# Attention scores of two query tiles as seven partial products, with another order of values and outputs

## The chip, the cores and the metric

The kernel runs on one core of one Trainium2 chip. It is a block of four layers (a gated linear attention, a feed-forward layer with 8-bit weights, a softmax attention, the same feed-forward layer again) on an input of 2 x 1024 tokens with 512 features, in float32. The metric is the device time of one execution in microseconds (us); lower is better. Three runs of the kernel before took 958.06, 958.42 and 961.21 us.

The core has a matrix engine (TensorE, PE in the profile; PEld is its weight load), a vector engine (VectorE, DVE), a scalar engine (ScalarE, ACT), GpSimd (POOL) and SyncE (SP), which issues most DMAs. Each works through its own instructions in order; semaphores make one wait for another. PSUM, the memory that TensorE writes, has eight banks of 128 x 512 float32.

## The reference

Only the third layer, the softmax attention, is touched. With `x` the normalised tokens:

```python
def _L0_attn_b_ref(x, W_q, W_k, W_v, W_o):
    scale = 1.0 / jnp.sqrt(jnp.asarray(x.shape[-1], x.dtype))
    Q = jnp.einsum('bsd,de->bse', x, W_q)
    K = jnp.einsum('bsd,de->bse', x, W_k)
    V = jnp.einsum('bsd,de->bse', x, W_v)
    scores = jnp.einsum('bqe,bke->bqk', Q, K) * scale
    attn = jax.nn.softmax(scores, axis=-1)
    out = jnp.einsum('bqk,bke->bqe', attn, V)
    return jnp.einsum('bse,ed->bsd', out, W_o)
```

Each of the two batches has 1024 tokens that attend to all 1024 tokens of their batch. The kernel folds the weights: with M = W_q W_k^T the scores are (x M) x^T, and with W_v W_o the last two products become one. So there are four products per batch: queries x M, scores, values x W_v W_o, outputs.

## The kernel before

Numbers are kept in two parts: a high part that TensorE's fast float32 format holds exactly, and a low part with the rest. `split` (L83) makes them: ScalarE casts the high part (L85), VectorE subtracts it for the low part (L86). A product of two such operands takes three matmuls, high x high, high x low, low x high (`mm3`, L95 to L98).

A batch has eight query tiles of 128 tokens and eight key tiles. `xTs[b, s]` holds half s of a batch's tokens transposed, 512 features as four blocks k of 128 partitions by 512 tokens, high and low part in one slot each. "Slots" are twelve buffers of 128 x 2048 (L39) shared by all stages. `wm` and `wvo` (L847 to L853) hold M and W_v W_o, loaded once from DRAM at the start of the stage.

- `q_proj` (L855) makes 512 queries: for each of four feature blocks 4 x 3 matmuls, split into `qh`, `ql`.
- `scores_b` (L874) makes the scores of one query tile: for each half of the keys 4 x 3 matmuls into one PSUM bank, the maximum of each half (L885), the negated scaled maximum `nm`, exponentials `pe` with their sums, the reciprocal `ri`.
- `probs_T` (L908) transposes the probabilities: VectorE transposes 32 x 32 blocks (L927), and a store to DRAM (`p_d`, L929) and four loads (L937) move the blocks to their places; then they are split into `pth` and `ptl`. The last tile of all is transposed on TensorE instead (L913 to L925).
- `out_b` (L946) makes the outputs of one tile, 8 x 3 matmuls, scales them by `ri`, adds the residual that it loads, and stores `x3`.
- `v_tile` (L958) makes 128 rows of values.

The order is written out in the loops at L986 to L1013: queries of the first half, four value tiles, scores of tile 0, four more value tiles, and then for each tile i the scores of i + 1, the probabilities of i and the outputs of i - 1. Other work is hung between: layer norms of the next tokens (`ln_steps`, which normalise, transpose in 32 x 32 blocks and move the blocks by DMA, L185 to L208), and the splits of the next tokens (`ln_split`, L210). `behind(last)` asks the scheduler to place such work after the last exponentials. The framework's scheduler then fixes each engine's order at build time.

The feed-forward layers already work by seven products. `combine` (L238) takes four quarters of the tokens of a pair of groups (B11, B12, B21, B22: two groups of 512 tokens by two halves of the features), forms the sums T1 to T4, and splits them; `products` (L304) multiplies them with prepared weights; in `ffn`, X, Y, Z and V are four PSUM banks that are added to each other on VectorE (L772 to L778) between the first four products and the last three. `ffn`'s second pass over layer "f" also carries the first norms and splits of the attention's tokens, given as its last argument (L838).

In the tail of each pass, `ffn` makes the outputs of eight token tiles: 22 matmuls each (L816, L817), a scaling and an addition on VectorE (L818, L819), a residual load before (L809) and a store after (L823). `xr` has two buffers.

## Time and profile before

| | |
|---|---|
| median of three runs | 958.42 us (958.06 to 961.21) |
| the profiled execution: its run, its span | 960.34 us, 958.5 us |
| TensorE busy (matmuls; weight loads) | 944.9 us (99%); 782.4 us (82%) |
| VectorE busy | 669.1 us (70%) |
| ScalarE busy | 372.6 us (39%) |
| GpSimd busy | 211.3 us (22%) |
| score matmuls `psc` | 384, 489.4 to 717 us |
| output matmuls `pob` | 384, 517.1 to 734.8 us |
| query and value matmuls `pqb`, `pvb` | 192 each |

The attention stage runs from about 463 to 735 us. The profile is one execution, taken by the hardware. In its rows the first number is the start or the sum of the busy time; matmul durations are from start to modelled end, and successive matmuls overlap. In a window's answer each engine has a pair: busy time and number of instructions, in the order PE, PEld, DVE, ACT, POOL, followed by the granted clock of TensorE, the share of the DMA engines and GB/s. A list of waits gives who waited on which line for whom, then the sum in us, how often, and the longest. The DMA share of the stage's window is 0.55.

### The profile page before, as it was taken

To read this page: it belongs to the slowest core of one execution; us is meant where nothing else is said; L and a number is where in the kernel's file an instruction comes from. 1 tells how busy PE (TensorE), PEld (TensorE's weight loads), DVE (VectorE), ACT (ScalarE), POOL (GpSimd) and SP (SyncE) were. 2 spreads that over 40 slices of the span, in tenths; PEclk is the share of its full clock that TensorE was granted. 3 is DMA by queue.
4 is the path that set the end of the run, shared out by engine and by line. 5 is a ranking of instruction groups with operands and counts; after the bars stand their busy time and mean duration, and the time that the engine had idled before them with its cause. 6 is when DMAs were issued, how large, how long until landed. Compare 5 with 4: busy or idle time off the path is not lost.

```text
span 958.5 us, 13125 instructions
## 1 busy us (share of the span) xinstructions
PE 944.9 (99%) x4450; PEld 782.4 (82%) x4450; DVE 669.1 (70%) x1361; ACT 372.6 (39%) x719; POOL 211.3 (22%) x310
## 2 busy tenths in 40 slices
PE   8999999999999999999999999999999999999998
PEld 7788788888888878888888877888888888888887
DVE  7766767768999699786437458246565986976655
ACT  4643424345565344454122224113233444434421
POOL 5432323333455011110001443104000121001100
PEclk9999999999999999999999999999999999999999
DMA  9536456574988457635505778427567762563112
GB/s 315 170 101 149 149 128 189 170 196 144 336 331 265 124 188 274 182 79 182 192 22 134 159 169 200 107 66 161 127 141 262 268 201 45 186 234 140 39 58 96
DMA packets 219250, 160.06 MB, mean 167 GB/s; under 512 B 154992, under 2 KB 170672, under 8 KB 219184
## 3 DMA queue, kind: packets, MB, share of 16 engines
q1 hardware_dynamic: 217136, 155.03, 54.1%
q0 software_dynamic: 2048, 4.20, 1.9%
q8 instruction: 35, 0.57, 0.2%
q14 instruction: 31, 0.25, 0.1%
HBM read 102.66 MB, written 41.84 MB: 151 GB/s over the span
## 4 chain that ended last, share of the span: by engine, by line
PE 65%; DMA 5%; DVE 5%; SPq 1%; POOL 1%; issue 0%; ACT 0%; DVEq 0%; ACTq 0%; POOLq 0%
PE pog L817 4%; PE pog L816 4%; PE pVg L312 4%; PE pZg L312 4%; PE pXg L312 4%; PE pVf L312 3%; PE pZf L312 3%; PE pXf L312 3%; PE pof L816 3%; PE pof L817 3%; PE pob L98 3%; PE pob L97 2%; PE pob L96 2%; PE psc L96 2%; PE psc L98 2%; PE psc L97 2%
## 5 line engine op out<-in xcount | busy, mean ns | idle before, releaser
L816 PE MATMUL pog<-wdg,hsg 128*128 128x512 f32 (+1 forms) x165 | 60.3, 375 | 0.0
L817 PE MATMUL pog<-wdg,hsg 128*128 128x512 f32 (+1 forms) x165 | 60.3, 376 | 0.0
L817 PE MATMUL pof<-wdf,hsf 128*128 128x512 f32 x154 | 59.4, 391 | 0.8 <-DVE hsf L86 0.8
L894 ACT ACTIVATE pe<-psc,nm 128x512 f32<-128x512 f32 x32 | 21.7, 684 | 98.1 <-DVE nm L889 98.1
L816 PE MATMUL pof<-wdf,hsf 128*128 128x512 f32 x154 | 59.2, 390 | 0.0
L98 PE MATMUL pob<-vh,ptl 128*128 128x512 f32 x128 | 50.3, 393 | 0.7 <-DVE ptl L86 0.7
L98 PE MATMUL psc<-xh_b,ql 128*128 128x512 f32 x128 | 50.6, 395 | 0.0
L96 PE MATMUL psc<-xh_b,qh 128*128 128x512 f32 x128 | 50.6, 395 | 0.0
L97 PE MATMUL psc<-xT_b,qh 128*128 128x512 f32 x128 | 50.5, 395 | 0.0
L96 PE MATMUL pob<-vh,pth 128*128 128x512 f32 x128 | 50.1, 392 | 0.2 <-ACT pth L85 0.2
L97 PE MATMUL pob<-vl,pth 128*128 128x512 f32 x128 | 49.9, 390 | 0.0
L86 POOL TENSOR_TENSOR hsg<-sgg,hsg 128x128 fp32r<-128x128 f32 x40 | 17.6, 462 | 146.0 <-ACT hsg L85 146.0
L117 POOL TENSOR_TENSOR rs_b<-ve_b,mhalf 128x1 f32<-128x1 f32 x16 | 10.9, 685 | 167.3 <-DVE ve_b L115 150.8
L312 PE MATMUL pVg<-T_g,wcg 128*128 128x512 f32 x176 | 46.9, 390 | 0.0
L312 PE MATMUL pVf<-T_f,wcf 128*128 128x512 f32 x176 | 46.6, 390 | 0.0
L312 PE MATMUL pXg<-B_g,wcg 128*128 128x512 f32 x176 | 46.6, 390 | 0.0
L312 PE MATMUL pXf<-B_f,wcf 128*128 128x512 f32 x176 | 46.0, 391 | 0.4 <-DMA wcf<-wc 0.4
L885 DVE TENSOR_REDUCE mx<-psc 128x1 f32<-128x512 f32 x32 | 21.9, 687 | 30.0 <-PE psc L98 29.8
L117 POOL TENSOR_TENSOR rs_g<-ve_g,mhalf 128x1 f32<-128x1 f32 x16 | 9.0, 573 | 144.7 <-DVE ve_g L115 128.2
L312 PEld LDWEIGHTS pXf<-B_f,wcf 128*128 128x128 f32 x176 | 32.9, 188 | 7.5 <-DMA wcf<-wc 0.8
L312 PEld LDWEIGHTS pVf<-T_f,wcf 128*128 128x128 f32 x176 | 33.1, 188 | 6.9
L312 PEld LDWEIGHTS pVg<-T_g,wcg 128*128 128x128 f32 x176 | 33.1, 188 | 6.9
(298 smaller groups left out, 2658.9 us busy)
## 6 DMA issues: line engine op xcount, KB each, us to landing
wcg<-wc SPq DMA_DIRECT2D x22, 896.0 KB, 5.4
wc<-wcf SPq DMA_DIRECT2D x11, 896.0 KB, 5.4
wcf<-wc SPq DMA_DIRECT2D x11, 896.0 KB, 6.1
p<-py SPq DMA_DIRECT2D x15, 512.0 KB, 3.4
ptl<-p SPq DMA_DIRECT2D x60, 128.0 KB, 3.1
xin_a<-in_x SPq DMA_DIRECT2D x16, 256.0 KB, 4.2
xra<-in_x SPq DMA_DIRECT2D x16, 256.0 KB, 3.5
row<-cl SPq DMA_DIRECT2D x16, 256.0 KB, 3.9
```

Of the source, the lines that this page charges most:

```text
L86: return c.ins, (eng or nc.vector).tensor_tensor(lo, src, hi.bitcast(F32), ALU.subtract).ins
L96: nc.tensor.matmul(ps, lhs_hi, rhs_hi, start=first, stop=False)
L97: nc.tensor.matmul(ps, lhs_hi, rhs_lo, start=False, stop=False)
L98: return nc.tensor.matmul(ps, lhs_lo, rhs_hi, start=False, stop=last).ins
L117: rsqrt[:] = [nc.gpsimd.tensor_tensor(rs, ve, mhalf, ALU.pow).ins]
L312: nc.tensor.matmul(ps, w[:, m, k * P : (k + 1) * P], o[:, s, k, :], start=first and k == 0 and s == 0, stop=k == 1 and s == 1, skip_group_ ...
L816: nc.tensor.matmul(ps, hs[i][0][:, j], wd[j][:, ds], start=j == 0, stop=False)
L817: nc.tensor.matmul(ps, hs[i][1][:, j], wd[j][:, ds], start=False, stop=j == KH - 1)
L885: nc.vector.tensor_reduce(mx[:, s : s + 1], ps, AX.X, ALU.max)
L894: nc.scalar.activation(pe[:, s * 512 : (s + 1) * 512], pS[s], AF.Exp, bias=nm, scale=SC, accum_out=rs[:, s : s + 1],).ins
```

## The change

A pair of query tiles (256 queries) is treated as a 2 x 2 block matrix: A11, A12 are the first tile's two halves of the features, A21, A22 the second tile's. The keys of a batch are the four quarters B11, B12, B21, B22, which `combine` prepares as it does for the feed-forward layers, for which a list of steps of its own is added for nm == "b" (with B12 split too, since queries and values read all four quarters). The eight block products become seven, P1 to P7:

- `q_proj` no longer splits: ScalarE copies the queries to float32 in a slot.
- `q_operands` forms S1 to S4 from the float32 queries on VectorE and splits A11, S1, S2, S3 (early) and A12, A22, S4 (late) into high and low parts, each 128 x 256.
- `scores_head` makes P1, P6, P5, P7 into X, Y, Z, V, and ScalarE and VectorE add them; `scores_tail` adds P2, P3, P4, and then takes the softmax of both tiles. One of the four score halves (`up`) now lies in SBUF.
- `cycle` is one pair's head, work in between, and tail. The order is new: in batch 0 all eight value tiles first, then the queries; in batch 1 the first queries, the outputs 5 to 7 of batch 0, then the values. `wvo` is loaded once per batch, ahead of `wm` in batch 0. Outputs run behind the next pair's scores.
- The tile that TensorE transposes is now the last but one; the last goes through DRAM.

```diff
@@ combine
+        if nm == "b":
+
+            return [
+                lambda: (begin(), part("B11", "B11")),
+                lambda: part("B21", "B21"),
+                lambda: part("B12", "B12"),
+                lambda: part("B22", "B22"),
+                lambda: less("B11", "B12", "B11"),
+                lambda: part("T1", "B11"),
+                lambda: less("B12", "B22", "B12"),
+                lambda: part("T3", "B12"),
+                lambda: less("B22", "B22", "B11"),
+                lambda: part("T2", "B22"),
+                lambda: less("B21", "B21", "B22"),
+                lambda: part("T4", "B21"),
+            ]
@@ ffn(x1, x2, "f", ...)
-        (ln_steps(x2, "b", 0) + ln_steps(x2, "b", 1), ln_split("b", 0) + ln_split("b", 1)),
+        (ln_steps(x2, "b", 0) + ln_steps(x2, "b", 1), combine("b", 0)),
@@ attention stage
+        def q_proj(b, g, ms):
+            if ms[0] == 0:
+                qs[b, g] = slot(f"q{b}{g}", F32).rearrange("p (k c) -> p k c", k=KD)
+            for m in ms:
...
+                nc.scalar.copy(qs[b, g][:, m, :], ps)
+        def q_operands(b, n, late):
...
+            def part(nm, src):
+                o = b1.tile([P, 2, 2, P], F32R, tag=f"op{nm}", name=f"op{nm}_{b}{n}")
+                QA[b, n, nm] = o
+                split(o[:, 0], o[:, 1], src)
+
+            if late:
+                part("A12", A["A12"])
+                part("A22", A["A22"])
+                nc.vector.tensor_tensor(A["A12"], A["A12"], A["A11"], ALU.subtract)
+                part("S4", A["A12"])
+                return
+            s1 = b1.tile([P, 2, P], F32, tag="s1", name=f"s1_{b}{n}")
+            part("A11", A["A11"])
+            nc.vector.tensor_tensor(s1, A["A21"], A["A22"], ALU.add)
+            nc.vector.tensor_tensor(A["A21"], A["A11"], A["A21"], ALU.subtract)
+            nc.vector.tensor_tensor(A["A11"], s1, A["A11"], ALU.subtract)
+            part("S2", A["A11"])
+            part("S1", s1)
+            part("S3", A["A21"])
+
+        def score_product(ps, b, n, nm, first):
+            a_, x = {
+                "P1": ("A11", "B11"), "P2": ("A12", "B21"), "P3": ("S4", "B22"), "P4": ("A22", "T4"),
+                "P5": ("S1", "T1"), "P6": ("S2", "T2"), "P7": ("S3", "T3"),
+            }[nm]
+            o, w = QA[b, n, a_], XT["b", b, x]
+            for k in range(2):
+                for i, j in ((0, 0), (0, 1), (1, 0)):
+                    nc.tensor.matmul(
                         ps,
+                        o[:, i, k],
+                        w[:, j, k],
+                        start=first and k == 0 and i + j == 0,
+                        stop=k == 1 and i == 1,
+                        skip_group_check=nm != "P6",
                     )
...
+        def scores_head(b, n):
+            X, Y, Z, V = (psum(f"ps{x}{b}{n}") for x in "XYZV")
+            for ps, nm in ((X, "P1"), (Y, "P6"), (Z, "P5"), (V, "P7")):
+                score_product(ps, b, n, nm, True)
+            u2 = b1.tile([P, 512], F32, tag="u2", name=f"u2b{b}{n}")
+            nc.scalar.copy(u2, X)
+            nc.vector.tensor_tensor(u2, Y, u2, ALU.add)
+            up = bp.tile([P, 512], F32, tag="up", name=f"upb{b}{n}")
+            nc.scalar.copy(up, Z)
+            nc.vector.tensor_tensor(Z, Z, u2, ALU.add)
+            nc.vector.tensor_tensor(V, V, u2, ALU.add)
+            nc.vector.tensor_tensor(up, V, up, ALU.add)
+            heads[b, n] = X, Z, V, up
+
+        def scores_tail(b, n):
+            X, Z, V, up = heads.pop((b, n))
+            for ps, nm in ((X, "P2"), (Z, "P3"), (V, "P4")):
+                score_product(ps, b, n, nm, False)
+            last.clear()
+            softmax(b * NK + 2 * n, (X, Z))
+            softmax(b * NK + 2 * n + 1, (V, up))
@@ probs_T
-            if t == NT - 1:
+            if t == NT - 2:
@@ order of the stage
+        def cycle(b, n, between):
+            scores_head(b, n)
+            if n == 0:
+                q_operands(b, 0, True)
+            if n < 3 and n != 1:
+                q_operands(b, n + 1, False)
+            between()
+            if n == 1:
+                q_operands(b, 2, False)
+            scores_tail(b, n)
+            if n < 3:
+                q_operands(b, n + 1, True)
+
+        wvo = blocks(vo_d, "wvo0_")
+        wm = blocks(m_d, "wm")
         for b in range(NB):
+            nm, src, g = ("b", x2, 2) if b == 0 else ("g", x3, 0)
+            norm = ln_steps(src, nm, g) + ln_steps(src, nm, g + 1)
             if b == 0:
+                for kt in range(NK):
+                    v_tile(0, kt)
+                do(norm, 4)
+                q_proj(0, 0, range(KD))
+                q_operands(0, 0, False)
+                do(norm, 4)
+            else:
+                do(moving, 1)
+                out_b(0, 5)
+                q_proj(1, 0, range(KD))
+                q_operands(1, 0, False)
+                do(moving, 4)
+                out_b(0, 6)
+                do(norm, 2)
+                out_b(0, 7)
+                wvo = blocks(vo_d, "wvo1_")
+                for kt in (4, 5, 6, 7):
+                    v_tile(1, kt)
+                do(moving, 2)
+                for kt in range(4):
+                    v_tile(1, kt)
+                do(norm, 2)
+                do(moving, 4)
+                do(norm, 4)
+            cycle(b, 0, lambda: q_proj(b, 1, (0, 1)))
+            do(norm, 2)
+            for i in (0, 1):
+                probs_T(b, i)
+            do(norm, 2)
+            cycle(b, 1, lambda: q_proj(b, 1, (2, 3)))
+            do(norm, 4)
+            for i in (2, 3):
+                probs_T(b, i)
+            out_b(b, 0)
+            if b:
+                moving = combine("g", 0)
+                do(moving, 2)
+            cycle(b, 2, lambda: out_b(b, 1))
+            for i in (4, 5):
+                probs_T(b, i)
+            out_b(b, 2)
+            if b:
+                do(moving, 2)
+            else:
+                moving = combine("b", 1)
+                do(moving, 1)
+            cycle(b, 3, lambda: out_b(b, 3))
+            if b == 0:
+                for i in (6, 7):
+                    probs_T(b, i)
+                out_b(b, 4)
+        do(moving, 3)
+        out_b(1, 4)
+        for i in (6, 7):
+            probs_T(1, i)
+        do(moving, 3)
+        out_b(1, 5)
+        out_b(1, 6)
         wcs = [stationary(n, "g0") for n in range(2)]
-        ended = (out_b(NB - 1, NK - 1),)
+        ended = (out_b(1, 7),)
```

In the names below, X, Y, Z, V are the four banks of a pair, an output's number is its query tile, and "head" and "tail" are the two functions above. `do` takes the next steps of a list and places them behind the last exponentials.

More of the change, by code (lines that the diff above doesn't have):

```diff
@@ L846, in hybrid_block_kernel @@
         bp = bctx.enter_context(tc.tile_pool(name="attn_b", bufs=2))
-        wm, wvo = [], []
-        for dst, d, n in ((wm, m_d, "wm"), (wvo, vo_d, "wvo")):
-            two = [slot(f"{n}{m}") for m in range(2)]
-            for k in range(KD):
-                w = two[k // 2][:, k % 2 * 1024 : (k % 2 + 1) * 1024]
-                nc.sync.dma_start(out=w.bitcast(F32), in_=d[k])
-                dst.append(w)
-        def q_proj(xT, name):
-            xh, xl = xT
-            qh = b1.tile([P, KD, 512], F32R, tag="qh", name=f"qh{name}")
-            ql = b1.tile([P, KD, 512], F32R, tag="ql", name=f"ql{name}")
-            for m in range(KD):
-                ps = psum(f"pqb{name}_{m}")
-                for k in range(KD):
-                    mm3(
-                        ps,
-                        wm[k][:, m * P : (m + 1) * P],
-                        wm[k][:, 512 + m * P : 512 + (m + 1) * P],
-                        xh[:, k, :],
-                        xl[:, k, :],
-                        k == 0,
-                        k == KD - 1,
-                    )
-                split(qh[:, m, :], ql[:, m, :], ps)
-            return qh, ql
@@ L874, in scores_b, with blocks @@
-        def scores_b(b, i):
-            t = b * NK + i
-            qh, ql = qTs[b, i // ST]
-            cs = bass.ts(i % ST, P)
-            pS = []
-            mx = mp.tile([P, 2], F32, tag="mx", name=f"mx{t}")
-            for s in range(2):
-                xh, xl = xTs[b, s]
-                ps = psum(f"psc{t}_{s}")
-                for k in range(KD):
-                    mm3(ps, qh[:, k, cs], ql[:, k, cs], xh[:, k, :], xl[:, k, :], k == 0, k == KD - 1)
-                nc.vector.tensor_reduce(mx[:, s : s + 1], ps, AX.X, ALU.max)
-                pS.append(ps)
+        def blocks(d, name):
+            two = [slot(f"{name}{m}") for m in range(2)]
+            w = [two[k // 2][:, k % 2 * 1024 : (k % 2 + 1) * 1024] for k in range(KD)]
+            for x, src in zip(w, d):
+                nc.sync.dma_start(out=x.bitcast(F32), in_=src)
+            return w
@@ new lines, in tokens @@
+        def tokens(b, g, k):
+            o = XT["b", b, f"B{k // 2 + 1}{g + 1}"]
+            return o[:, 0, k % 2], o[:, 1, k % 2]
+        def q_proj(b, g, ms):
+            if ms[0] == 0:
+                qs[b, g] = slot(f"q{b}{g}", F32).rearrange("p (k c) -> p k c", k=KD)
+            for m in ms:
+                ps = psum(f"pqb{b}{g}_{m}")
+                ms_ = slice(m * P, (m + 1) * P), slice(512 + m * P, 512 + (m + 1) * P)
+                for k in range(KD):
+                    mm3(ps, wm[k][:, ms_[0]], wm[k][:, ms_[1]], *tokens(b, g, k), k == 0, k == KD - 1)
+                nc.scalar.copy(qs[b, g][:, m, :], ps)
@@ new lines, in q_operands @@
+        def q_operands(b, n, late):
+            A = {}
+            for i in range(2):
+                for j in range(2):
+                    c = (n % 2 * 2 + i) * P
+                    A[f"A{i + 1}{j + 1}"] = qs[b, n // 2][:, 2 * j : 2 * j + 2, c : c + P]
+            def part(nm, src):
[16 more added lines that the diff above has]
+            part("S3", A["A21"])
@@ new lines, in scores_tail, with softmax @@
+        def scores_tail(b, n):
[5 more added lines that the diff above has]
+            softmax(b * NK + 2 * n + 1, (V, up))
+        def softmax(t, halves):
+            mx = mp.tile([P, 2], F32, tag="mx", name=f"mx{t}")
+            for s, x in enumerate(halves):
+                nc.vector.tensor_reduce(mx[:, s : s + 1], x, AX.X, ALU.max)
@@ L891, in scores_b @@
             rs = mp.tile([P, 2], F32, tag="rsum", name=f"rsum{t}")
-            for s in range(2):
-                last[:] = [
-                    nc.scalar.activation(
-                        pe[:, s * 512 : (s + 1) * 512],
-                        pS[s],
-                        AF.Exp,
-                        bias=nm,
-                        scale=SC,
-                        accum_out=rs[:, s : s + 1],
-                    ).ins
-                ]
+            for s, x in enumerate(halves):
+                act = nc.scalar.activation(
+                    pe[:, s * 512 : (s + 1) * 512], x, AF.Exp, bias=nm, scale=SC, accum_out=rs[:, s : s + 1]
+                )
             ri = mp.tile([P, 1], F32, tag="ri", name=f"ri{t}")
             nc.vector.tensor_tensor(ri, rs[:, 0:1], rs[:, 1:2], ALU.add)
-            last.append(nc.vector.reciprocal(ri, ri).ins)
+            last[:] = act.ins, nc.vector.reciprocal(ri, ri).ins
             pes[t] = pe, ri
@@ L958, in v_tile @@
         def v_tile(b, kt):
-            xh, xl = xTs[b, kt // ST]
             cs = bass.ts(kt % ST, P)
@@ L962, in v_tile @@
             for k in range(KD):
+                xh, xl = tokens(b, kt // ST, k)
                 w = wvo[k]
-                mm3(ps, xh[:, k, cs], xl[:, k, cs], w[:, 0:512], w[:, 512:1024], k == 0, k == KD - 1)
+                mm3(ps, xh[:, cs], xl[:, cs], w[:, 0:512], w[:, 512:1024], k == 0, k == KD - 1)
             h_ = b1.tile([P, 512], F32R, tag=f"vh{kt}", name=f"vh{b}_{kt}")
@@ L968, in v_tile @@
             vs[b, kt] = h_, l_
-        xTs, qTs, pes, ptT, vs, last = {}, {}, {}, {}, {}, []
-        fill = [[[] for _ in range(NK)] for b in range(NB)]
-        for b, src, nm, g, its in (
-            (0, x2, "b", 2, (0, 0, 1, 1, 1, 1, 2, 2)),
-            (0, x2, "b", 3, (2, 2, 3, 3, 3, 3, 4, 4)),
-            (0, x3, "g", 0, (5, 5, 6, 6, 7, 7, 7, 7)),
-            (1, x3, "g", 1, (0, 0, 1, 1, 1, 1, 2, 2)),
-        ):
-            for t, step in zip(its, ln_steps(src, nm, g)):
-                fill[b][t].append(step)
@@ L981, in hybrid_block_kernel, with do @@
-        fill[0][6][:0] = ln_split("b", 2)
-        moving = combine("g", 0)
-        for n in range(10):
-            fill[1][(3, 3, 4, 4, 4, 5, 5, 5, 6, 6)[n]].append(moving.pop(0))
+        qs, QA, heads, pes, ptT, vs, last = {}, {}, {}, {}, {}, {}, []
+        def do(steps, n):
+            with behind(last):
+                for _ in range(n):
+                    steps.pop(0)()
+        def cycle(b, n, between):
[10 more added lines that the diff above has]
+                q_operands(b, n + 1, True)
@@ L986, in hybrid_block_kernel @@
+        wvo = blocks(vo_d, "wvo0_")
+        wm = blocks(m_d, "wm")
         for b in range(NB):
+            nm, src, g = ("b", x2, 2) if b == 0 else ("g", x3, 0)
+            norm = ln_steps(src, nm, g) + ln_steps(src, nm, g + 1)
             if b == 0:
-                xTs[0, 0], xTs[0, 1] = lnT["b", 0], lnT["b", 1]
-            qTs[b, 0] = q_proj(xTs[b, 0], f"{b}_0")
-            if b > 0:
-                out_b(b - 1, NK - 1)
-            for kt in range(4):
-                v_tile(b, kt)
@@ L994, in hybrid_block_kernel @@
-            if b > 0:
-                for step in ln_split("b", 2 * b + 1):
-                    step()
-            xTs[b, 1] = lnT["b", 2 * b + 1]
-            scores_b(b, 0)
-            for kt in range(4, 8):
-                v_tile(b, kt)
-            for i in range(NK):
-                with behind(last):
-                    for step in fill[b][i]:
-                        step()
-                if i + 1 < NK:
-                    scores_b(b, i + 1)
-                if i == 2:
-                    qTs[b, 1] = q_proj(xTs[b, 1], f"{b}_1")
-                probs_T(b, i)
-                if i > 0:
-                    out_b(b, i - 1)
-                if b + 1 < NB and i == 6:
-                    xTs[b + 1, 0] = lnT["b", 2 * b + 2]
+                for kt in range(NK):
+                    v_tile(0, kt)
```

## The prediction

> **What bounds the kernel now.** First the page's row of engine shares, then one window over the attention stage (463 to 735 us, from its first query matmul to the first product of the last feed-forward part):

> ```profile
> 463.00:735.00 272.00, 271.09 (x1185) 221.32 (x1184) 145.04 (x293) 69.84 (x143) 50.82 (x80) 1.00 0.55 134
> ```

> TensorE (first pair) is busy throughout at granted clock 1.00; VectorE, the third pair, is busy 145.0 us, 53%. So the stage ends when TensorE has issued its matmuls, and only two things count: how many there are, and whether one waits. The price of one comes from the timeline:

> ```profile
> 463.12 0.39 PE L96 MATMUL pqb<-xh_b,wm 128*128 128x512 f32 x1
> 463.35 0.39 PE L97 MATMUL pqb<-xT_b,wm 128*128 128x512 f32 x1
> 463.57 0.39 PE L98 MATMUL pqb<-xh_b,wm 128*128 128x512 f32 x1
> ```

> The second column (0.39) is start to end; starts are 0.227 us apart. The waits of TensorE's weight loads name what stops it in this stage:

> ```profile
> PEld pob L98 <- DVE ptl L86: 1.9, 3, 1.1
> ...
> PEld pob L96 <- ACT pth L85: 0.7, 1, 0.7
> ```

> Both are an output product waiting for its transposed probabilities: 2.6 us in all.

> **What is removed.** A pair of query tiles now takes 7 products x 2 k x 3 parts = 42 matmuls instead of 2 x 24. Eight pairs save 48. [...] With the 2.6 us of named waits replaced by the new ones below: -13.5.

> **What is added on VectorE and ScalarE.** Queries: 16 `ql` rows (0.684) go; 88 operations on 128x256 come. The trace has none of this line; the nearest is a two-tensor operation on 128x256:

> ```profile
> L818 DVE TENSOR_TENSOR og<-pog,sd_b 128x256 f32<-128x256 f32 x2 | 0.8, 425 | 3.0 <-PE pog L817 3.0
> ```

> 88 x 0.425 - 10.9 = +26.5. Assembly of the scores: 32 x 0.685 = +21.9. Keys: 16 parts and 8 differences of 128x1024 at 1.215 instead of 16 splits at 0.679 = +18.3. Together +66.7, about 9 of it in the feed-forward tail before: 145 + 58 = 203 us in some 258, 79%. In sum that fits beside TensorE; in rows VectorE's operations overlap by about 0.08 (two statistics take 1.28, the next starts after 1.20), so I price 0.605 for 512 wide, 0.345 for 256, 1.14 for 1024. ScalarE gets 56 casts of 128x256 (0.405, between 0.297 for 128 columns and 0.62 for 512), 16 copies (0.587) and wider key casts (16 x 1.05 for 16 x 0.62): 70 becomes about 105. Neither is a bound by its sum; what costs is the order in which waits stand in their queues.

> **Waits, taken from the instruction order of the changed program.**

> (a) *Stage start.* Before, the weights came early; their loads stood ahead of the last residual loads:

> ```profile
> 451.08 3.15 SPq L852 DMA_DIRECT2D wvo<-vo  x4
> ...
> 465.14 0.38 SPq L823 DMA_DIRECT2D x<-xrf  x1
> 468.23 0.32 SPq L809 DMA_DIRECT2D xrf<-x  x1
> ```

> The last two lines are tile 13's store and tile 15's load: the load waits for the store to land (3.1 us), as they share a buffer. Now all of `wvo` stands in SP's queue behind this pair, and the first `v_tile` matmul needs it; queued behind that matmul are all others. Tile 13's store waits for VectorE, where between tile 13's scaling (458.1) and its addition stand the last hidden split (1.6), a difference, T3's low part (1.14 each), a statistic and a transpose (0.6 each): 465.2 if VectorE is never late; adding up its queue from 436.9 gives 467.0. Then 3.1 + 0.4, and landing (3.4 us for a 512 KB `p`, 3.8 at best for `wm`): 472 to 474. TensorE is through with the feed-forward products at 463.1 + 22 x 0.227 = 468.1. Cost 4 to 6, taken **5.0**; ends 0.5 (VectorE early, no wait on the store) and 9 (landing as `wvo`'s 8.6). `wm` follows 21.8 us of value matmuls later and is hidden.

> (b) *First head of each batch.* P2 into X must wait for ScalarE's copy of X, which stands behind three casts: X's P1 is done at 1.4 us after the query products, the copy at 2.35. **1.0** in batch 0; in batch 1 values precede, and only T2's cast is late, **0.5**. Ends 0.5 and 4.

> (c) *First output.* From pair 0's last P3 to its probabilities: maximum, negation, the ACT table load (1.28), behind a cast that waits for P4, two exponentials, 128x1024 transpose: 5.7. Then the round trip through DRAM, seen here:

> ```profile
> 522.96 1.23 DVE L927 STREAM_TRANSPOSE py<-pe 128x1024 f32<-128x1024 f32 x1
> ```
> ```profile
> 535.15 1.14 ACT L85 CAST pth<-ptl 128x512 fp32r<-128x512 f32 x2 [3.25 <-DMA ptl<-p]
> ```

> 11.0 from end to start; the clean ones of the trace take 7.5 and 7.8, the worst 14.4. I take 8.8 (landing 3.4, issues 2.3, landing 3.1) and 0.6 for the cast: 15.1 in all. Before output 0, TensorE has 60 matmuls = 13.6. Stall **1.5**; batch 1 has no table load: 14.0 against 14.4, 0. Ends 0 and 7.

> (d) *Third output, pair 1.* Its negated maximum stands in VectorE's queue behind tile 1's low split, which waits for a DMA, and some 20 rows (8 x 0.605 + 9 x 0.345 + 2.1): 10.1 after output 0 began. Exponentials, then ten rows before the transpose: 14.3. Its store stands behind a residual load that waits for x3's store: +0.6; 8.8 + 0.6: ready at 24.3. TensorE has 84 matmuls = 19.0, and waits 0.8 there for Z's addition: **5.2** together. Batch 1: ready at 22.6, TensorE at 20.3 with 1.2 waited: **3.5**. Ends 1 and 14.

> (e) Later pairs have 96 matmuls (21.8) of cover for chains of 17; the very last tile now goes through DRAM and is ready within 1 us of its turn, 0.5; the tail before, with 3 more us of VectorE on a queue nearly full, 0.5. **1.0**, ends 0 and 6. `wvo`'s second load has 8 us of cover, and POOL's DMAs stand at the same points as the cover: nothing.

> (f) *Clock.* No named wait of TensorE in the trace is above 1.8 us, and the clock is 1.00 in every slice. [...] Taken **1.0**.

> Sum: 5.0 + 1.5 + 1.5 + 8.7 + 1.0 + 1.0 = 18.7; -13.5 + 18.7 = **+5.2**. Against the profiled execution: span 958.5 becomes 963.7, its run 960.3 becomes 965.5. The three runs shown have median 958.4, so I forecast 963.5.

> [...]

> **Rivals.** *TensorE stays fed* (faster): round trips as the clean 7.5, `wvo` landing at the floor, the scheduler's order leaving only (a) 4 and 1 elsewhere: -13.5 + 5 = -8.5, **950**. For it: interleaved score and output products give every queue something else; against it: in-order engines stop on the first wait. It decides once all new waits stay under 10.6 us. *Even* (within 0.3%): clean round trips, no clock loss: 4 + 1.5 + 0.2 + 6.1 + 1 = 12.8, -0.7, **957.7**. *VectorE becomes the bound* (slower): if its 111 rows from pair 0's operands to Z's addition of pair 2 don't overlap, they take 53.4 us against TensorE's 48.9, and my 44.5 grows by 8.9 in batch 0, some 5 in batch 1: **977**. For it: 79% is a mean over dense and empty stretches; against: the overlap shows in every dense stretch. *It doesn't do what it says*: 42 matmuls per pair stand in the built order; under 1%.

> **Chances.** Forecast (waits of 11 to 25 us) 0.42, VectorE bound 0.14, even 0.17, fed 0.27. A difference of 0.3% (2.9 us) is about what a measurement here can tell: faster 0.27, same 0.17, slower 0.56. The forecast's own range is 960 to 972; to hold 8 in 10 it must reach the fed case at 950 and, above, half of the VectorE case: 950 to 975. The ends of all waits together (2 to 44) would give 947 to 989.

> **What would show it.** 336 matmuls of score products and starts 0.227 apart; the first value matmul some 5 us after the last feed-forward one, released by DMA `wvo`; waits of `pob` for `pth` of about 4 us before the third output of each batch; VectorE near 205 us. Wrong: `wvo` landed before TensorE gets there, `pob` waits under 3 us in sum, or VectorE named as the releaser of score products for over 5 us.

## The result, and the profile after

The changed kernel takes **970.0 us** (median of six runs, 965.6 to 972.7) against 958.5 for the kernel before (six runs, 957.8 to 961.2). The ratio is 1.0113, with an interval of 1.0086 to 1.0140: slower. The profiled execution, the slowest of the six, has a span of 970.8 us against 958.5, so 12.3 us have to be accounted for, where the prediction had 5.2.

The stage after, as one window from the last feed-forward product (469.2) to the first product of the next layer (742.9), in the same columns as before, then two rows of the page (busy share and granted clock in 40 slices of 24.3 us):

```profile
469.20:742.90 273.70, 261.53 (x1115) 211.21 (x1114) 188.38 (x390) 102.86 (x216) 49.82 (x78) 0.98 0.58 149
```
```profile
PE   8999999999999999999899989999999999999998
...
PEclk9999999999999999999899999999999999999999
```

TensorE is no longer busy throughout: 261.5 of 273.7 us, and the granted clock is 0.98. VectorE has 188.4 us, 69% of the stage, and is not the bound. From the list of waits (who, line, for whom: us in sum, how often, the longest), the matmul engine's own in the changed part:

```profile
PE pob L96 <- ACT pth L85: 6.3, 4, 3.1
...
PE pvb L96 <- DMA wvo<-vo: 4.8, 1, 4.8
...
PE pVg L328 <- DVE upg L794: 1.9, 1, 1.9
...
PE psX L926 <- ACT u2b L940: 0.8, 1, 0.8
```

The first two and the last were forecast. The third, in the feed-forward layer behind the stage, was not. But what these gaps set off is larger than any one of them. The timeline of TensorE at the start of the stage:

```profile
469.19 0.39 PE L833 MATMUL pof<-wdf,hsf 128*128 128x512 f32 x1
474.34 0.80 PE L96 MATMUL pvb<-wvo,B_b 128*128 128x512 f32 x1 [4.77 <-DMA wvo<-vo]
474.93 0.63 PE L97 MATMUL pvb<-wvo,B_b 128*128 128x512 f32 x1
475.36 0.63 PE L98 MATMUL pvb<-wvo,B_b 128*128 128x512 f32 x1
475.79 0.63 PE L96 MATMUL pvb<-wvo,B_b 128*128 128x512 f32 x1
...
478.98 0.40 PE L98 MATMUL pvb<-wvo,B_b 128*128 128x512 f32 x1
```

After 4.77 us of standing still, matmuls start 0.43 us apart instead of 0.227 until 478.7. Windows of 3.41 us, the length of the shortest stretch at half clock in this profile, laid over this place (the third number from the right is the granted clock):

```profile
468.46:471.87 3.41, 1.11 (x5) 0.57 (x4) 3.41 (x6) 1.05 (x1) 0.00 (x0) 1.00 0.37 110
471.87:475.28 3.41, 0.94 (x2) 0.83 (x3) 3.03 (x8) 0.00 (x0) 0.93 (x2) 0.50 0.94 359
475.28:478.69 3.41, 3.41 (x9) 2.64 (x8) 2.37 (x4) 0.00 (x0) 0.55 (x1) 0.50 1.02 380
478.69:482.10 3.41, 3.41 (x16) 2.76 (x15) 0.00 (x0) 0.00 (x0) 0.00 (x0) 1.00 0.98 377
```

A window in which TensorE was busy for 1.11 us is followed by one at half clock, one with 0.94 us by another, one with 3.41 us by full clock. The same happens at 564.0, 697.2 and 792.7 us, and at 215.9 us, in a part that the change doesn't touch. The five stretches last 3.41 us or twice that, and they start whole multiples of 3.413 us apart (471.87 to 564.03 is 27 of them, 215.87 to 471.87 is 75).

**The 12.3 us**, by the gaps of the profile. A gap costs 0.16 us more than its named idle time, as idle is counted from a matmul's modelled end (0.39 us) where the next would have started after 0.227. A half-clock stretch is priced at half of the time in it in which TensorE works, as matmuls start 0.43 us apart there and 0.227 outside.

| | us |
|---|---|
| 48 matmuls fewer, at 0.227 | -10.9 |
| waits of before's stage that are gone (0.24 and 0.67, twice 0.16) | -1.2 |
| start of the stage, `wvo` | +4.9 |
| first heads, `u2` and T2 | +1.4 |
| four waits of outputs for `pth` (0.91, 3.08, 0.33, 2.02) | +7.0 |
| `pVg` in the next layer | +2.0 |
| half clock behind four of these gaps (2.2, 1.5, 1.7, 1.7) | +7.1 |
| before the changed part (half clock at 216 us) | +1.9 |
| sum | +12.2 |

The last row but one is the accident of one execution: a gap of 2.00 us there, where the profile before shows 1.39 and 1.59 at the same products, and no half clock.

How did `pVg`'s wait come about? SyncE's and VectorE's timelines at the end of the stage (the second number is the issue or the operation, not the transfer):

```profile
734.87 1.40 SPq L317 DMA_DIRECT2D wcg<-wc  x3
736.99 0.32 SPq L1017 DMA_DIRECT2D xrb<-x  x1
```
```profile
747.15 0.75 DVE L1021 SCALAR_TENSOR_TENSOR xrb<-pob,ri,xrb 128x512 f32<-128x512 f32 x1 [1.49 <-DMA xrb<-x]
...
788.86 0.71 DVE L195 STREAM_TRANSPOSE y_g<-xn_g 128x512 f32<-128x512 f32 x1 [5.46 <-DMA xT_g<-y_g]
```

The last output's residual (256 KB) was issued 0.7 us after three weight loads of 896 KB and took 10.1 us to land. VectorE adds it at 747.15, 4.3 us after the next layer began, where before it was 0.2 us. Its queue then carries the lateness to the norms' single buffer `y`, and at 790 us TensorE waits for it.

### The profile page after: what moved, and what is told of

Read it like the earlier page. It is cut to its first block, busy times and chain, and to the rows that moved or that the text cites. A ratio compares the mean times of both kernels' runs of the same rounds, so it can differ in the third digit from the quotient of the medians.

```text
span 970.8 us, 13238 instructions
## 1 busy us (share of the span) xinstructions
PE 943.2 (97%) x4402; PEld 777.9 (80%) x4402; DVE 722.3 (74%) x1473; ACT 408.5 (42%) x791; POOL 213.5 (22%) x310
## 4 chain that ended last, share of the span: by engine, by line
PE 72%; DVE 10%; DMA 9%; SPq 4%; issue 2%; ACT 2%; POOL 1%; DVEq 0%; POOLq 0%; ACTq 0%
PE pog L833 4%; PE pog L832 4%; PE pXg L328 4%; PE pVg L328 4%; PE pZg L328 4%; PE pVf L328 3%; SPq L205 3%; PE pZf L328 3%; PE pXf L328 3%; PE pob L96 2%; PE pob L98 2%; PE pob L97 2%; PE pYg L328 2%; PE psX L926 2%; PE pvb L96 2%
## 5 line engine op out<-in xcount | busy, mean ns | idle before, releaser
L96 PE MATMUL pob<-vh,pth 128*128 128x512 f32 x128 | 50.8, 397 | 6.3 <-ACT pth L85 6.3
L97 PE MATMUL pob<-vl,pth 128*128 128x512 f32 x128 | 50.2, 392 | 0.0
L98 PE MATMUL pob<-vh,ptl 128*128 128x512 f32 x128 | 50.0, 391 | 0.0
L86 POOL TENSOR_TENSOR hsg<-sgg,hsg 128x128 fp32r<-128x128 f32 x40 | 17.7, 463 | 143.2 <-ACT hsg L85 143.2
L117 POOL TENSOR_TENSOR rs_b<-ve_b,mhalf 128x1 f32<-128x1 f32 x16 | 12.9, 810 | 144.6 <-DVE ve_b L115 144.5
L328 PEld LDWEIGHTS pXg<-B_g,wcg 128*128 128x128 f32 x176 | 34.1, 194 | 7.3
L832 PEld LDWEIGHTS pog<-wdg,hsg 128*128 128x128 f32 x165 | 31.1, 188 | 5.7
L833 PEld LDWEIGHTS pog<-wdg,hsg 128*128 128x128 f32 x165 | 31.0, 188 | 5.6
L96 PEld LDWEIGHTS pob<-vh,pth 128*128 128x128 f32 x128 | 24.1, 189 | 13.3 <-ACT pth L85 8.4
L833 PEld LDWEIGHTS pof<-wdf,hsf 128*128 128x128 f32 x154 | 28.9, 188 | 6.8 <-DVE hsf L86 0.8
```

What stands on the lines that cost most here:

```text
L86: return c.ins, (eng or nc.vector).tensor_tensor(lo, src, hi.bitcast(F32), ALU.subtract).ins
L96: nc.tensor.matmul(ps, lhs_hi, rhs_hi, start=first, stop=False)
L97: nc.tensor.matmul(ps, lhs_hi, rhs_lo, start=False, stop=False)
L98: return nc.tensor.matmul(ps, lhs_lo, rhs_hi, start=False, stop=last).ins
L117: rsqrt[:] = [nc.gpsimd.tensor_tensor(rs, ve, mhalf, ALU.pow).ins]
L328: nc.tensor.matmul(ps, w[:, m, k * P : (k + 1) * P], o[:, s, k, :], start=first and k == 0 and s == 0, stop=k == 1 and s == 1, skip_group_ ...
```

## The experiments

The runs were made in four groups, each with the kernel before beside it: its median was 960.0 us beside e1 to e4, 958.6 beside e5 to e7 and beside e8 to e10, 959.4 beside e11 and e12, and 958.5 beside the changed kernel. A difference of medians between two groups is therefore uncertain by about 1.5 us. Where it matters, the difference of the ratios to the kernel before is given too.

**e1: the values' weight earlier.** `blocks` moves ahead of the feed-forward layer, and one of its tail's hidden steps issues the load:

```diff
...
+    wvo = []
+    parts = combine("b", 0)
+    step = parts[8]
+    parts[8] = lambda: (step(), wvo.extend(blocks(vo_d, "wvo0_")))
-        (..., combine("b", 0)),
+        (..., parts),
...
...
-        wvo = blocks(vo_d, "wvo0_")
```

> The changed kernel with one edit: the first load of W_v W_o is issued with the tail's eighth... ninth hidden step, ahead of tile 12's store, instead of behind tile 13's store and tile 15's residual load. Theory A (the queue in front of the load makes the 4.8 us wait of the first value matmul, and the 4.3 us of matmuls at half clock behind it follow from that gap): no wait on wvo, granted clock 1.00 from 470 to 480 us, and 4.8 + 2.2 = 7 us less: 963 against 970.0. Rival B (2 MB of wvo in the tail delay the residual loads and stores there, so that the wait only changes its name): 967 to 970. Rival C (clock falls for another reason than the gap): 965, with the slow stretch still there.

963.4 us (ten runs, 960.6 to 968.3), 6.6 less than the changed kernel (7.3 by the ratios): theory A. The load is issued at 458.1, values begin at 465.0 between the last feed-forward products, and nothing waits for `wvo`. The waits of outputs grew, though (10.0 us in e1's profile, in five places, against 6.3).

**e2: the residual ahead of the next weights.**

```diff
...
-        wcs = [stationary(n, "g0") for n in range(2)]
         ended = (out_b(1, 7),)
+        with behind((res[NT - 1],)):
+            wcs = [stationary(n, "g0") for n in range(3)]
```

> The changed kernel with one edit: the three loads of the next feed-forward layer's weights (896 KB each) are issued behind the last output's residual load instead of ahead of it. Theory A (that load took 10.1 us because 2.7 MB went ahead of it; VectorE, 1.5 us late there and 4 us in all, then reaches the moves of the next norms late, and that makes the wait of pVg on upg at 790 us and the half clock behind it): the residual lands in under 4 us, no wait of pVg above 0.5 us near 790, 1.9 + 1.6 = 3.5 us less: 966.5 against 970.0. Rival B (the moves of the norms are late by the queue of SyncE and the single buffer y alone): the pVg wait stays, 970. Rival C (the first weights of the layer come late instead): a wait of pXg on wcg of 1 to 4 us at the start of the layer, 970 to 973.

969.5 us (968.3 to 973.9): no gain that four runs can tell, so A's 966.5 did not come. The profile shows the change in waits that A named. VectorE's addition now waits for TensorE instead of the load, and `pVg` doesn't wait:

```profile
743.15 0.75 DVE L1021 SCALAR_TENSOR_TENSOR xrb<-pob,ri,xrb 128x512 f32<-128x512 f32 x1 [4.12 <-PE pob L98]
```

But this profile has two waits that the one of the changed kernel had not: 1.26 us of the last outputs for `pth` (e12's profile of the changed kernel has it too, 1.30), and 0.94 us for `wcg`, rival C in part. The edit comes back in e9. One profile speaks less plainly: in e11 the same load lands late (9.7 us) and VectorE waits 1.1 us for it, but `pVg` doesn't wait; there TensorE had just waited 2.07 us for its weights.

**e3: the first gap filled.** The load is as late as before, but TensorE has 20 matmuls whose result is not used:

```diff
...
+                with behind((endmm[0],)):
+                    fill("s", 20)
                 for kt in range(NK):
                     v_tile(0, kt)
```

> The changed kernel with 20 matmuls of 128x512 on tokens that are ready, their result unused, between the last feed-forward matmul and the first value matmul: the 4.8 us gap is filled with 4.5 us of work, the load of W_v W_o is as late as before. Theory A (the clock falls because TensorE stood still): the clock stays at 1.00 there, the value matmuls start 0.227 apart at once, 2.2 us less: 967.8 against 970.0. Rival B (the first value matmuls are slow by the load still landing beside them): starts stay 0.43 apart for ten matmuls, 970.

966.7 us (963.9 to 968.3), 3.3 less than the changed kernel (5.0 by the ratios), where A had 2.2. The timeline of TensorE there:

```profile
468.66 4.70 PE L1049 MATMUL fills<-B_b 128*128 128x512 f32 x20
473.59 0.50 PE L96 MATMUL pvb<-wvo,B_b 128*128 128x512 f32 x1 [0.23 <-DMA wvo<-vo]
473.92 0.39 PE L97 MATMUL pvb<-wvo,B_b 128*128 128x512 f32 x1
474.15 0.40 PE L98 MATMUL pvb<-wvo,B_b 128*128 128x512 f32 x1
474.39 0.39 PE L96 MATMUL pvb<-wvo,B_b 128*128 128x512 f32 x1
```

With the gap filled, the values come 0.23 us apart from the second on, though the same loads still land beside them: the slow stretch came from standing still, not from the load.

**e4: the kernel before with 42 matmuls a pair.**

```diff
-                for k in range(KD):
+                for k in range(KD // 2 if i % 2 and s else KD):
```

> The kernel before with 6 of the 48 score matmuls of each pair of tiles left out (half the features in the second key half of each odd tile, so these scores are not the reference's), nothing else changed. Theory A (each matmul is worth its 0.227 us): 48 x 0.227 = 10.9 us less, 947.5 against 958.4. Rival B (waits behind TensorE come up as soon as it has less to do: ptl, pth): 950 to 955.

948.2 us, 11.8 less than the kernel before in its group; the ratio is 0.9875 (0.9856 to 0.9894), that is 10.2 to 13.8 us less. The 10.9 us lie within this: the matmuls are worth their pitch if nothing else changes.

**e5: eight products in the new order**, with e1's early load: `combine` makes only the four quarters, `q_operands` the four parts, the head P1, P3, P5, P7 and the tail the rest into the same four banks.

```diff
...
-                "P1": ("A11", "B11"), "P2": ("A12", "B21"), "P3": ("S4", "B22"), "P4": ("A22", "T4"),
-                "P5": ("S1", "T1"), "P6": ("S2", "T2"), "P7": ("S3", "T3"),
+                "P1": ("A11", "B11"), "P2": ("A12", "B21"), "P3": ("A11", "B12"), "P4": ("A12", "B22"),
+                "P5": ("A21", "B11"), "P6": ("A22", "B21"), "P7": ("A21", "B12"), "P8": ("A22", "B22"),
...
```

> The kernel of e1 (values' weight early) with the scores in eight products, all else of the new order kept: no T1 to T4, no S1 to S4, no additions between head and tail; 48 matmuls per pair. Its matmuls cost 10.9 us more than those of e1 (963.4). Theory A (the output waits come mainly from the work that seven products bring to VectorE and ScalarE): the waits of pob on pth of pairs 1 and of psX on u2 (3.1 + 2.5 + 0.8 us in e1) go, 963.4 + 10.9 - 6.4 = 968. Rival B (they are the round trip through DRAM and would come with any products in this order): 974, with pob waits above 2 us as in e1. Rival C (all waits of the attention go, 10 us or more, and none is left that seven products would not bring back): 962 to 964.

969.0 us (968.2 to 972.0), about what A has (968). Its list of waits has one of an output for `pth`, against e1's five:

```profile
PE pob L96 <- ACT pth L85: 4.7, 1, 4.7
```

So most output waits come with the seven products, from what they add on VectorE and ScalarE or from the six matmuls of cover that they take from each pair (the two were not parted), and not from the round trip alone. In this order the seven products bring 969.0 - 963.4 = 5.6 of their 10.9 us (6.7 by the ratios).

**e6: every output one place later**, on e1.

```diff
...
-            out_b(b, 0)
-            cycle(b, 2, lambda: out_b(b, 1))
+            cycle(b, 2, lambda: out_b(b, 0))
...
-            out_b(b, 2)
+            out_b(b, 1)
-            cycle(b, 3, lambda: out_b(b, 3))
+            cycle(b, 3, lambda: out_b(b, 2))
...
```

> The kernel of e1 with each output one place later (output 0 in the middle of pair 2, output 1 behind it, and so on; 24 more matmuls, 5.4 us, between a tile's probabilities and its outputs). Theory A (the third output waits for a chain that is a fixed 22 to 24 us long against 19 us of matmuls): pob waits on pth of pair 1 (3.1 and 2.5 us) go, no half clock from them, 963.4 - 6 = 957. Rival B (the moved outputs delay what they free, so the wait moves to the next tiles): 961 to 965, with pob waits of 2 to 4 us at other outputs.

972.7 us, 9.3 more than e1: the waits moved, as rival B said, but the time is worse than its 961 to 965. That later outputs free their buffers later is a possible reason; it was not tried by itself. In batch 0 an output waits longer than any in e1, and in batch 1 a head now waits for its operands:

```profile
580.89 0.80 PE L96 MATMUL pob<-vh,pth 128*128 128x512 f32 x1 [4.94 <-ACT pth L85]
...
675.28 0.79 PE L929 MATMUL psY<-T_b,opS 128*128 128x512 f32 x1 [3.00 <-ACT opS L85]
```

**e7: tile 2 of each batch transposed on TensorE**, on e1.

```diff
...
-            if t == NT - 2:
+            if t in (2, NK + 2, NT - 2):
...
-            for i in (2, 3):
-                probs_T(b, i)
-            cycle(b, 2, lambda: out_b(b, 1))
+            cycle(b, 2, lambda: (out_b(b, 1), probs_T(b, 2), probs_T(b, 3)))
```

> The kernel of e1 with tiles 2 of both batches transposed on TensorE (8 transposes, 1.0 us by the trace) in the middle of pair 2, and tile 3's probabilities behind it, instead of the round trip through DRAM (9.4 us). Theory A (the round trip is what makes the third output late): the waits before the third outputs go, 963.4 - 3.1 - 2.5 + 2 x 1.0 - 1 of clock = 959. Rival B (what is late is the negated maximum in VectorE's queue, not the trip): the wait turns into one of the transposes on ScalarE's exponentials, 962 to 964. Rival C (tile 3, now later, waits instead): pob waits on pth of 2 to 4 us before the fourth output, 963 to 966.

962.5 us (956.4 to 963.9), 0.9 less than e1, which is within the spread of both. A is right about the third outputs: they no longer wait. But now the last output does, which none of the three theories named, and then the clock falls (0.50 from 725.95 to 729.36 us):

```profile
725.74 0.63 PE L96 MATMUL pob<-vh,pth 128*128 128x512 f32 x1 [4.42 <-ACT pth L85]
```
```profile
712.85 1.08 SPq L317 DMA_DIRECT2D wcg<-wc  x2
716.36 6.34 SPq L1007 DMA_DIRECT2D ptl<-p  x4
```

The second fence is SyncE's queue: the four loads of tile 15's probabilities stand behind 1.8 MB of weights and take 6.3 us to issue, against 2.2 to 3.5 us for such a four in the changed kernel.

**e8, e9, e10.** e8 adds tile 15 (`NT - 1`) to e7's list, e9 is e8 with e2's edit, e10 is e8 with e5's.

> The kernel of e7 with tile 15 transposed on TensorE too (as 14 is): in e7 its loads from DRAM stood behind 1.8 MB of the next layer's weights, the last output waited 4.4 us, and 3.4 us at half clock followed. Theory A (these two are lost time): 962.5 - 4.4 - 1.7 + 1.0 = 957.4, with a profile of 954 to 956. Rival B (the next layer then starts earlier and waits for its weights instead): 960 to 962, with pXg waiting on wcg for 2 to 5 us.

> The kernel of e8 with the edit of e2 as well (the next layer's weights behind the last residual load). Theory A (weights ahead of small loads in the DMA queues cost where the end of the stage waits for them; nothing waits in e8 once the tiles are transposed on TensorE): the same as e8 within 1 us. Rival B: 2 to 4 us less than e8, as the residual's lateness delays VectorE in the next layer. Rival C: 1 to 3 us more, by later weights.

> The kernel of e8 with the scores in eight products, as in e5. Theory A (with the order's waits mended, 48 matmuls more cost nearly their full 10.9 us): e8 + 9 to 11, so 966 to 968. Rival B (the seven products still cost waits of their own, u2 and the additions): e8 + 4 to 7, 961 to 964.

| | median us (runs) | ratio to before (interval) |
|---|---|---|
| e8 | 957.0 (12) | 0.9981 (0.9965 to 0.9996) |
| e9 | 953.8 (6) | 0.9945 (0.9927 to 0.9963) |
| e10 | 961.4 (12) | 1.0025 (1.0013 to 1.0037) |

e8 is A, and **e9 is faster than both kernels**, 4.7 us under the median of before. Of its theories rival B holds, 3.2 us less than e8, with intervals that just don't meet. Which wait the runs of e8 had and those of e9 had not, the two profiles don't show: their spans are 952.1 and 953.0, but the profiled execution of e8 was its fastest and that of e9 its slowest. In e9's list, what is left of the output waits (the 0.8 us for `u2` stays):

```profile
PE pob L96 <- ACT pth L85: 1.3, 3, 0.8
```

e10 is rival B: eight products cost 4.4 us more than seven, not 10.9. The two profiles say where the rest went. Their spans differ by 5.6 us, so 5.3 us of the saving are missing. From 440 us to the end e10 has no gap of 0.22 us or more, and e8 has seven: 2.4 us for `u2`, T2 and `pth` in the stage and 1.9 us for weights and Z in the next layer, 5.4 us with 0.16 for each. And e10, with as many products as the kernel before and no such waits, is still 2.9 us slower than it: it makes 24 more transposes on TensorE (4.0 us in its profile, 1.0 before). That this is the whole of the 2.9 us is an estimate from these two numbers, not a trial.

**e11 and e12.** e11 is e3 with 12 and 8 more such matmuls before the third outputs; e12 is the changed kernel again.

> The changed kernel as in e3, and with 12 and 8 more unused matmuls before the third outputs of the two batches, where it stood still for 3.1 and 2.0 us: three of its four long gaps are filled with 4.5 + 2.7 + 1.8 us of work that lengthens none of them. Theory A (the gaps cost their own length, and half as much again by the clock): 970.0 - 2.2 - 1.5 - 1.7 = 964.6, no half clock in the attention stage. Rival B (the clock costs little, e3 gained by chance): 967 or more.

> The changed kernel unaltered, on the same chip as e11, for the spread of its time. If the half clock comes by the phase of fixed windows of 3.41 us against the gaps, executions differ by steps of 1.7 us and their time follows their mean granted clock: 963 to 973, median 970.

e12: 972.5 us (967.5 to 974.1), 1.0122 (1.0102 to 1.0143), mean clock 0.991 to 0.995. The time goes with the clock only roughly: the fastest execution has the highest, but one at 0.991 took 971.3 us and two at 0.993 took 972.4 and 972.6. e11: 970.6 us (966.8 to 973.1), clock 0.996 to 1.000. So the clock is mostly back, and the median has moved by 1.9 us only, with intervals that overlap: A falls as a forecast of the time. In e11's profiled execution (span 965.3) the attention has no half clock. Its first two long gaps are filled (0.41 and 0.40 us are left), but before the third output of batch 1 TensorE still stands still for 1.72 us after the 8 matmuls: that gap was not filled. And the next layer waits for its weights, and the clock falls there (0.50 from 784.35 to 787.76 us):

```profile
782.91 0.47 PE L331 MATMUL pXg<-B_g,wcg 128*128 128x512 f32 x1 [2.07 <-DMA wcg<-wc]
```

Three of e11's six executions took over 972 us at clock 0.996 to 1.000. They were not profiled, so where their time went stays open.

## Why the prediction came out as it did

Sign, range and mechanism held: seven products save 10.9 us, and new waits take more than that. The range alone says little, as 950 to 975 reaches from 8 us faster to 17 us slower. The size was off by 7.1 us in the profiled execution (6.4 by the medians), and would have been off by more if two errors had not offset each other: the outputs' waits were put 3.2 us too high, the clock 6.1 us too low. By the prediction's own steps:

| step | forecast | measured |
|---|---|---|
| removed matmuls, 48 at 0.227 between starts | -10.9 | -10.9 (e4 agrees) |
| removed waits | -2.6 | -1.2 |
| (a) stage start | 5.0 | 4.9 |
| (b) first heads | 1.5 | 1.4 |
| (c), (d) outputs | 10.2 | 7.0 |
| (e) last tile and tail | 1.0 | 2.0, in another place |
| (f) clock | 1.0 | 7.1 |
| untouched part | 0 | 1.9 |

**(f) is the step that failed, by its size.** No run shows the 1.0; it was the author's estimate, where the profile before has clock 1.00 in every slice and no wait of TensorE above 1.8 us. Measured were four stretches in the changed part that cost 1.5 to 2.2 us each, 7.1 together. 1.85 us of idle TensorE in a window of 3.41 was enough for the shortest of these gaps, `pVg`'s; in these profiles what decides is how much of such a window TensorE stands still (the counts are in the last section). e3 shows the link between gap and clock at the first of them. That all 7.1 us come back when the gaps are filled is not shown: e11 regained 1.9.

**(a)** held to 0.1 us, for the reason given: tile 13's store was issued at 468.24, after VectorE had been busy for all of the 27.2 us from 442.0 to 469.2. **(d)** was right in its place and late by the right queue (the negated maximum of tile 2 came at 551.6, 9.7 us after output 0 began, forecast 10.1), but exponentials and transpose followed sooner: the transpose began 12.6 us after output 0 instead of 14.3. The round trip from the transpose's end to the cast took 8.2 us for tile 0 and 8.1 for tile 2, near the 8.8 taken. **Removed waits**: 2.6 was the list of the weight loads; the matmuls themselves stood still 0.9 us, and that list was the one to take.

**(e)** put 0.5 each on the feed-forward tail and the last tile, both with little. What came instead was the residual load behind the next layer's weights. The prediction looked at the order of the queues at the start of the stage, for `wvo`, and not at its end, where the new order let 2.7 MB go ahead of 256 KB. In e2's profile, without that order, the wait is gone; one profile with the late load and without the wait (e11) leaves room for another part in it.

Rivals: VectorE was not the bound. Its whole busy time rose from 669.1 to 722.3 us, by 53 and not the 67 of the sum.

## What to carry to other kernels

When a change takes work off the engine that sets the end, count its new gaps one by one, and price each at its length plus the chance of a half-clock stretch behind it (1.5 to 2.2 us each here). A saving of 48 matmuls was given back by four gaps of 1.9 to 4.8 us. Look at the end of the changed stage as at its start: small loads that stand behind the next stage's weights can come late there (10.1 us here, 256 KB behind 2.7 MB). And more distance between a producer and its reader is no sure cure (e6 lost 9 us); a shorter chain was, for the outputs that it served (e7's third ones, and in e8 no output waited for more than 0.7 us).
